# Loading the first matrices in halves, the last expert's tokens in halves, and stages placed anew, in a two-layer attention and expert kernel

## The chip, the cores and the metric

The kernel runs on one core of one Trainium2 chip, in one launch. The metric is the device time of a run in microseconds, lower is better. A core has five instruction queues that run side by side and wait for each other by semaphores: PE (TensorE, matrix products into PSUM), DVE (VectorE), ACT (ScalarE), POOL (GpSimd) and SP (SyncE, here only for issuing transfers). ACT and POOL can issue transfers as well. In the trace, PEld is the loading of PE's weights, which lies beside the products.

## The reference

Eight sequences of 512 tokens with 256 channels (4096 tokens in all) pass through four residual steps, and every step first normalizes its input:

```
x = x + attention0(norm(x), ctx)      # 8 heads of 64, context of 64 tokens with 192 channels, masked
x = x + experts0(norm(x))             # 16 experts of 64, the best 4 of each token, sigmoid weights
x = x + attention1(norm(x), ctx)      # 4 heads of 32, the best 32 keys, FiLM, long convolution, an MLP of 1024, norms
x = x + experts1(norm(x))             # 8 experts of 1024; each takes the 512 tokens that score it highest
```

What the change touches at the start is in attention0: keys are `ctx @ W_k`. The kernel folds queries and keys into one matrix for each sequence and head, `M0 = W_q[head] @ k[head].T`, so that scores are `x @ M0`. What it touches at the end is experts1:

```
vals, idx = top_k(scores.T, 512)          # 512 tokens for each expert
h = gelu(norm(x[idx]) @ fc1 + b1)         # 256 -> 1024
o = (h @ fc2 + b2) * weight               # 1024 -> 256
out = x.at[idx].add(o)                    # added to the tokens' rows
```

## The kernel before

All data is float32. Tokens lie on the 128 partitions; a sequence is 4 tiles of 128 tokens. A program product of float32 shows in the trace as two PE instructions.

**Loads at the start (L341 to L364).** ACT's queue issues `ctxT` (96 partitions, 2 blocks c of 96 channels, 512 columns: 384 KiB), then `wqT` (512 KiB), the mask and `bo`. SP's queue issues `wk` (384 KiB, in `places`), `xT(0)`, `x(0)`, and then weights in the order of need. The trace shows SP and ACT issuing the ninth and later loads only as earlier ones land. DVE forms the sums of `wqT` and scales it (L366 to L369).

**Keys (L371 to L377).** For each block m of 128 of the 512 key rows, `from_context(wk, m)` multiplies the two halves of the context's channels (c = 0 and 1) into one PSUM bank of `ps_m` (two pools of two banks), and ACT (m even) or DVE (m odd) copies it into `kT`. L378 to L385 then form `M0` from `wqT` and `kT` in products of 64 rows.

**The middle (L1310 to L1377).** The four steps of each sequence b are Python generators: `attend0`, `route0`, `experts0`, `attend1`, `convolve`, `dense1`, `settle`, `offer`; `build` prepares the convolution's kernel, mostly on DVE. A list `parts` gives each generator a number of steps and a start and an end in planner's units, and `emit` sorts all steps of all generators by these times. That order is the program's order, from which the framework's scheduler makes each engine's queue; instructions passed to `keep_in_program_order` (called `pin` in the code) keep their order among themselves. `experts0` asks for the routing weights `wB`, spread over the partitions by a transfer, and DVE multiplies them with the products at L803. In `convolve`, DVE's L1059 makes `yv` from the products.

**The last step (L1383 to the end).** A search on DVE and PE finds each expert's tokens. For every expert e, POOL gathers the rows (L1500) and PE transposes them. PE then multiplies with `fc1` in 8 blocks f (`inner`, L1529) and ACT applies GELU from PSUM into `gT` (L1559), at 512 tokens each. For each quarter q of 128 tokens, PE multiplies `gT` with `fc2` (L1562), DVE adds the bias (L1564) and scales (L1565), and POOL adds the rows to `out` by an indirect transfer (L1566). Expert 0 already has its first four blocks in halves of 256 columns, and those are pinned.

Of the kernel before, what the change touches and what calls it, by code (L numbers as in the profile page):

```python
# [21 lines left out]
P = 128  # L22
# [37 lines left out]
def xattn_ffn_two_layers(ctx: ExitStack, tc: tile.TileContext, a: dict, out: bass.AP):  # L60
# [19 lines left out]
    def ps_m(i=None):  # L80
        if i is None:
            turn[0] += 1
            i = turn[0] % 2
        return pm[i].tile([P, 512], F32, name="ps_m")

    def ps_o():
        return po.tile([P, 512], F32, name="ps_o")

    def load(p, name, src, shape, dtype=F32, eng=None):
        t = p.tile(shape, dtype, name=name)  # L90
        (eng or nc.sync).dma_start(t, src)
        return t
# [104 lines left out]
    def mm(ps, pairs):  # L197
        n = len(pairs)
        for i, (lhsT, rhs) in enumerate(pairs):
            nc.tensor.matmul(ps, lhsT, rhs, start=(i == 0), stop=(i == n - 1))  # L200
# [137 lines left out]
    a0t = pool(sl, "a0_t", 2)  # L338
    sv = ExitStack()
    wp = pool(sv, "a0_v")  # L340
    ctxT = load(wp, "ctxT", a["ctxT"].rearrange("(c p) s -> p c s", c=2), [96, 2, B * SC], eng=nc.scalar)  # L341

    wk = places[:96, 12].rearrange("p (c n) -> p c n", c=2)
    nc.sync.dma_start(wk, a["Wk0"].rearrange("(c p) n -> p c n", c=2))
    wqT = places[:, 13].rearrange("p (c n) -> p c n", c=4)
    nc.scalar.dma_start(wqT, a["WqT0"].rearrange("(c p) n -> p c n", p=P))
    load_xT(0)
    load_x(0)
    wv = load(wp, "wv", a["Wv0"].rearrange("(c p) n -> p c n", c=2), [96, 2, 512])
# [21 lines left out]
    def from_context(w, m, i=None):  # L371
        ps = ps_m(i)
        mm(ps, [(w[:, c, m * P : (m + 1) * P], ctxT[:, c, :]) for c in range(2)])
        return ps

    for m in range(4):
        (nc.vector.tensor_copy if m % 2 else nc.scalar.copy)(kT[:, m, :], from_context(wk, m))  # L377
    for hp in range(H0 // 2):  # L378
        for dq in range(2):
            for g in range(2):  # L380
# [412 lines left out]
    def experts0(b):  # L793
        xb = xs[b]
        xT, wBs = routed.pop(b)

        def first(f):
            if f in (2, 4):
                wBs.append(spread(b, len(wBs)))
            wB = wBs[f // 2][:, f % 2]  # L800
            ps = ps_m(1)
            mm(ps, [(keys[:, k, f * P : (f + 1) * P], xT[:, k, :]) for k in range(2)])
            nc.vector.scalar_tensor_tensor(wB, ps, 0.0, wB, ALU.max, ALU.mult)  # L803
            return wB

        for i, acc in enumerate((yield from two_layers(first, vals))):
            pair = xb[:, 2 * i : 2 * i + 2, :]
            nc.vector.tensor_tensor(pair, acc, pair, ALU.add)
            for j in (2 * i, 2 * i + 1):
                n_a1.rows(xb[:, j, :], b * TPB + j)  # L810
        n_a1.close(b)
        nc.sync.dma_start(midr[:, tiles(b), :], xb)
# [413 lines left out]
    def once(action):  # L1226
        action()
        yield
# [92 lines left out]
    for b in range(B):  # L1321
        parts += [
            (attend0(b), 10, b + -0.111, b + 1.0),
            (route[b], 2, b + 1.025, b + 1.04),
            (route[b], 2, b + 1.135, b + 1.601),
            (experts0(b), 17, b + 1.936 + -0.015 * max(b - 5, 0), b + 2.436 + -0.015 * max(b - 5, 0)),
        ]
        if b >= 3:
            parts.append((staged(b), 1, b - 0.9, b - 0.9))
        if b >= 2:  # L1330
            parts.append((staged_T(b), 1, b - 0.6, b - 0.6))
    parts += [(once(convolving), 1, 8.01, 8.01), (once(dense), 1, B + 1.52, B + 1.52)]

    early = (5.5, 7.184, 8.7)
    for b in range(B):
        t = T2 + b
        u = early[b] if b < 3 else t
        v = (8.1, 8.66, 9.952)[b] if b < 3 else t + 1
        n = 0.5 if b < 3 else 1.0
        parts += [  # L1340
            (attends[b], 2, u + -0.02, u + 0.182),
            (attends[b], 8, u + 0.249, u + 0.681),
            (attends[b], 8, u + 0.681, u + 0.938),
            (attends[b], 1, u + 0.933, u + 0.933),
            (attends[b], 1, v - 0.05, v - 0.05),
            (attends[b], 1, v - 0.03, v - 0.03),
            (convs[b], 1, v + 0.035, v + 0.035),
            (convs[b], 4, v + 0.224 * n, v + 0.5 * n),
            (convs[b], 3, v + 0.512 * n, v + 0.605 * n),
            (convs[b], 4, v + 0.597 * n, v + 0.819 * n),  # L1350
        ]
        if b < B - 1:
            parts += [
                (denses[b], 1, t + 2.7, t + 2.7),
                (denses[b], 17, t + 2.718, t + 3.6),
                (settle(b), 5, t + 3.628, t + 3.815),
                (offers[b], 1, t + 4.1 - 0.25 * (b == B - 2), t + 4.1 - 0.25 * (b == B - 2)),
                (offers[b], 1, t + 4.179 - 0.25 * (b == B - 2), t + 4.179 - 0.25 * (b == B - 2)),
            ]
        else:  # L1360


            u = t + 2.46
            parts += [
                (dense1(b, 0), 18, u, u + 0.624),
                (settle(b, 0), 3, u + 0.65, u + 0.65 + 0.05),
                (offer(b, 0), 2, u + 0.72, u + 0.72 + 0.05),
                (dense_last(b, 1), 12, u + 0.61, u + 0.61 + 0.624),
            ]
            for j in js_of(1):  # L1370
                v = u + 0.61 + 0.624 + 0.1 * (j - 2)
                parts += [
                    (settle(b, (j,)), 2, v + 0.01, v + 0.03),
                    (offer(b, (j,)), 2, v + 0.04, v + 0.06),
                ]
    parts.append((once(ending), 1, T2 + B + 1.946, T2 + B + 1.946))
    emit(parts)  # L1377
    s2r.close()

# [130 lines left out]
    for e in range(NE1):  # L1510
        f1, f2 = ns.fcs.pop(e)
        if 0 < e < NE1 - 1:
            lists[e + 1] = listed(e + 1)
        idx, ys = lists.pop(e)

        def affine(dst, src, k):
            nc.scalar.activation(  # L1517
                dst, src, AF.Identity, bias=ns.bet[:, k : k + 1], scale=ns.gam[:, k : k + 1]
            )

        yT = place("yT", e).rearrange("p (k j) d -> p k (j d)", k=2)
        gT = (places[:, 4:8] if e % 2 else places[:, 16:20]).rearrange("p s (f n) -> p (s f) n", n=CAP)
        pss = {}

        def inner(f, cols):
            if f not in pss:
                pss[f] = ps_m()
            for k in range(2):
                ins = nc.tensor.matmul(  # L1529
                    pss[f][:, cols], f1[:, k, f * P : (f + 1) * P], yT[:, k, cols], start=(k == 0), stop=(k == 1)  # L1530
                )
                if cols.stop - cols.start < CAP:
                    pin(ins)

        if e:
            transposed(2, yT, ys, affine)
        else:

            halves = [slice(0, CAP // 2), slice(CAP // 2, CAP)]
            banks = [ps_t(k) for k in range(2)]  # L1540
            for i, cols in enumerate(halves):
                for j in (2 * i, 2 * i + 1):
                    for k, ps in enumerate(banks):
                        y = ys[j][:, k * P : (k + 1) * P]
                        pin(nc.tensor.transpose(ps[:, j * P : (j + 1) * P], y, ident))
                    if j < 2:
                        awake(2)
                for k, ps in enumerate(banks):
                    affine(yT[:, k, cols], ps[:, cols], k)
                for f in range(4):  # L1550
                    inner(f, cols)
            placed(slice(1, NE1))
            lists[1] = listed(1)
        for f in range(NF):
            if f not in pss:
                inner(f, slice(0, CAP))
            ps = pss.pop(f)
            c = e * NF + f
            nc.scalar.activation(gT[:, f, :], ps, AF.Gelu_apprx_tanh, bias=ns.bb1[:, c : c + 1])  # L1559
        for q in range(NQ):  # L1560
            pso = ps_o()
            mm(pso[:, :D], [(gT[:, f, q * P : (q + 1) * P], f2[:, f, :]) for f in range(NF)])  # L1562
            o = wk2.tile([P, D], F32, name="o", bufs=2 * NQ)
            nc.vector.tensor_tensor(o, pso[:, :D], ns.bb2[:, e, :], ALU.add)  # L1564
            nc.vector.tensor_scalar(o, o, ys[q][:, D + e : D + e + 1], None, ALU.mult)  # L1565
            nc.gpsimd.indirect_dma_start(  # L1566
                out=out,
                out_offset=bass.IndirectOffsetOnAxis(ap=idx[:, q : q + 1], axis=0),
                in_=o,
                in_offset=None,  # L1570
                compute_op=ALU.add,
            )
        if e + 2 < NE1:
            ns.fcs[e + 2] = fc_weights(e + 2)
# [124 lines left out]
```

## Time and profile before

| what | us |
|---|---|
| median of 3 runs (lowest, highest) | 1286.02 (1284.69, 1287.09) |
| the profiled execution, its time | 1283.47 |
| its span, first to last instruction | 1281.7 |
| PE busy | 1156.5 (90%) |
| DVE busy | 796.9 (62%) |
| POOL busy | 568.4 (44%) |
| ACT busy | 396.3 (31%) |
| mean granted PE clock | 0.963 |
| wait for the first load at the start | 6.85 |
| last scatter issued at | 1273.85 |

The profile is one execution. Busy shares are means over stages that have different limits, and a busy PE is not a PE at its peak. In a line of the timeline the first number is the start and the second the busy time of the group in it, then engine, line, operation, what it writes and reads, and in brackets the idle time ahead of it and what ended that. In a line of waits stand the total, the number of times and the longest. A line of windows has the busy time and number of instructions of PE, PEld, DVE, ACT and POOL, then the granted PE clock, the share of the DMA engines and GB/s.

### The profile page before, as it was taken

The page shows a single profiled execution, that of the slowest core. Times are in us where ns is not written, and L with a number is a line of the kernel's source. Part 1 is how long each engine was busy: PE and PEld are TensorE (multiplying, and loading weights), DVE is VectorE, ACT ScalarE, POOL GpSimd, SP SyncE. Part 2 cuts the span into 40 slices and gives each one's busy share as a digit, 9 for nine tenths or more (in the row PEclk, how much of TensorE's full clock was granted, in tenths as well). Part 3 has the DMA queues.
Part 4 walks back from the last instruction along what each step waited for, and adds up shares of the span by engine and source line. Part 5 has one row for each costly group of instructions (what it writes and reads, how often), then busy time and mean ns, then how long its engine had stood idle before and what let it go on. Part 6 is the DMA issues. An engine that isn't in the chain of part 4 may idle for free. (4 is left out here: it accounts for less than half of the span.)

```text
span 1281.7 us, 17161 instructions
## 1 busy us (share of the span) xinstructions
PE 1156.5 (90%) x5563; PEld 737.6 (58%) x5563; DVE 796.9 (62%) x3340; ACT 396.3 (31%) x784; POOL 568.4 (44%) x809
## 2 busy tenths in 40 slices
PE   7998989979899989998789999898977799999995
PEld 3555655646566546564445556464655576666663
DVE  4459958847987884698987889795435612211110
ACT  2332222131312330223246355634352022222220
POOL 2333324332342333455596477849763123333331
PEclk9998989989889989999898999999998899999998
DMA  8003314315030223200001101022221024443321
GB/s 256 18 28 84 86 49 115 84 51 132 2 100 11 74 75 84 95 1 17 1 1 50 50 1 35 17 63 72 86 71 34 17 59 115 117 103 100 99 38 17
DMA packets 60783, 80.32 MB, mean 63 GB/s; under 512 B 6035, under 2 KB 45204, under 8 KB 60566
## 3 DMA queue, kind: packets, MB, share of 16 engines
q1 hardware_dynamic: 53142, 69.26, 18.4%
q0 software_dynamic: 6240, 8.79, 4.1%
q10 hardware_dynamic: 1312, 1.18, 0.3%
q8 instruction: 44, 0.72, 0.2%
q14 instruction: 45, 0.37, 0.1%
HBM read 62.04 MB, written 17.17 MB: 62 GB/s over the span
## 5 line engine op out<-in xcount | busy, mean ns | idle before, releaser
L261 PE MATMUL ps_o<-vals,wB 128*128 128x256 f32 x512 | 127.9, 395 | 10.6 <-DVE wB L803 10.6
L200 PE MATMUL ps_m<-xT,keys 128*128 128x512 f32 x256 | 126.2, 620 | 0.0
L261 PEld LDWEIGHTS ps_o<-vals,wB 128*128 128x128 f32 x512 | 98.0, 197 | 38.6 <-DVE wB L803 15.2
L200 PE MATMUL ps_m<-hT,w 128*128 128x512 f32 (+1 forms) x256 | 116.1, 576 | 0.2 <-ACT hT L1084 0.2
L261 PE MATMUL ps_o<-w,gT 128*128 128x256 f32 x480 | 114.4, 380 | 0.1
L1529 PE MATMUL ps_m<-places 128*128 128x512 f32 (+1 forms) x272 | 113.9, 570 | 0.5 <-ACT places L1517 0.5
L200 PE MATMUL ps_o<-places 128*128 128x256 f32 x512 | 114.0, 379 | 0.1
L1566 POOL DMA_INDIRECT out<-o,idx x32 | 51.5, 1610 | 141.0 <-DVE o L1565 73.5
L200 PEld LDWEIGHTS ps_o<-places 128*128 128x128 f32 x512 | 96.6, 190 | 18.4 <-issue 5.7
L261 PEld LDWEIGHTS ps_o<-w,gT 128*128 128x128 f32 x480 | 89.7, 190 | 28.1 <-issue 14.9
L1564 DVE TENSOR_TENSOR o<-ps_o,bb 128x256 f32<-128x256 f32 x32 | 13.6, 425 | 147.1 <-PE ps_o L200 147.1
L972 DVE MATCH_REPLACE8 places<-top,places 128x64 f32<-128x64 f32 x512 | 101.3, 205 | 0.0
L705 POOL TENSOR_TENSOR sc<-sc,mx 128x512 f32<-128x512 f32 x32 | 33.2, 1045 | 119.6 <-DVE mx L704 84.4
L156 DVE BATCH_NORM_STATS2 bnst<-places 128x6 f32<-128x256 f32 x192 | 72.8, 413 | 21.3 <-POOL places L1156 12.8
L1559 ACT ACTIVATE places<-ps_m,bb 128x512 f32<-128x512 f32 x64 | 44.0, 687 | 126.8 <-PE ps_m L1529 126.8
L1529 PEld LDWEIGHTS ps_m<-places 128*128 128x128 f32 x272 | 51.1, 191 | 51.1 <-issue 48.8
L971 DVE MAX8 top<-places 128x8 f32<-128x64 f32 x512 | 79.3, 208 | 0.1
L1042 POOL TENSOR_TENSOR places<-places,t 128x768 f32<-128x768 f32 x32 | 57.5, 1821 | 48.1 <-DVE t L1034 48.0
L200 PEld LDWEIGHTS ps_m<-xT,keys 128*128 128x128 f32 x256 | 49.7, 201 | 43.6 <-issue 40.7
L803 DVE SCALAR_TENSOR_TENSOR wB<-ps_m,wB 128x512 f32<-128x512 f32 x64 | 43.4, 679 | 46.0 <-PE ps_m L200 45.9
L191 PE MATMUL ps_t<-ident,places 128*128 128x128 f32 x256 | 49.4, 288 | 24.8 <-DVE places L722 7.9
L1096 ACT ACTIVATE gT<-ps_m,b 128x512 f32<-128x512 f32 (+1 forms) x64 | 42.1, 657 | 90.4 <-PE ps_m L200 90.1
(369 smaller groups left out, 2238.6 us busy)
## 6 DMA issues: line engine op xcount, KB each, us to landing
wB<-wd SPq DMA_DIRECT2D x64, 256.0 KB, 4.3
places<-in_fc2T SPq DMA_DIRECT2D x8, 1024.0 KB, 5.5
places<-in_fc1T SPq DMA_DIRECT2D x8, 1024.0 KB, 4.9
xT<-in_xT SPq DMA_DIRECT2D x8, 512.0 KB, 3.5
places<-in_x SPq DMA_DIRECT2D x8, 512.0 KB, 3.9
mid_x<-places SPq DMA_DIRECT2D x8, 512.0 KB, 7.2
places<-mid_x SPq DMA_DIRECT2D x8, 512.0 KB, 6.5
tab<-zt SPq DMA_DIRECT2D x7, 528.0 KB, 3.9
```

What stands on the lines that cost most here:

```text
L156: nc.vector.bn_stats(st, src)
L191: nc.tensor.transpose(ps[:, j * P : (j + 1) * P], r[:, k * P : (k + 1) * P], ident)
L200: nc.tensor.matmul(ps, lhsT, rhs, start=(i == 0), stop=(i == n - 1))
L261: nc.tensor.matmul(acc[j // 2][:, (j % 2) * D : (j % 2 + 1) * D], h[:, j * P : (j + 1) * P], rhs[:, f, :], start=(f == 0 and j % 2 == 0), ...
L803: nc.vector.scalar_tensor_tensor(wB, ps, 0.0, wB, ALU.max, ALU.mult)
L971: nc.vector.max(m8, src[:, h, :])
L972: nc.vector.match_replace(wrk[:, h, :], m8, src[:, h, :], -FMAX)
L1042: nc.gpsimd.tensor_tensor(ts[0][:, i], ts[0][:, i], ts[1][:, i], op)
L1096: nc.scalar.activation(g, ps, AF.Gelu, bias=ns.b1[:, f : f + 1])
L1529: ins = nc.tensor.matmul(pss[f][:, cols], f1[:, k, f * P : (f + 1) * P], yT[:, k, cols], start=(k == 0), stop=(k == 1))
L1559: nc.scalar.activation(gT[:, f, :], ps, AF.Gelu_apprx_tanh, bias=ns.bb1[:, c : c + 1])
L1566: nc.gpsimd.indirect_dma_start(out=out, out_offset=bass.IndirectOffsetOnAxis(ap=idx[:, q : q + 1], axis=0), in_=o, in_offset=None, compute ...
```

## The change

Three things are changed. First, `ctxT` and `wk` are each loaded by two transfers, one for each c, the first halves first on ACT's and on SP's queue; `wqT` is split in two, one half on each queue, behind them. The four key banks are opened together, and the products run over all m with c = 0 and then over all m with c = 1, pinned in that order; the copies come after. Second, the last expert (e = 7) makes its first layer on the left 256 tokens for all 8 blocks, then on the right 256 tokens for two blocks, then quarter 0, then the other six right blocks, then quarters 1 to 3, all products pinned; GELU runs on 256 columns there. The other experts keep their form. Third, 14 or so of the planner's numbers are changed.

```diff
-    ctxT = load(wp, "ctxT", a["ctxT"].rearrange("(c p) s -> p c s", c=2), [96, 2, B * SC], eng=nc.scalar)
+    ctxT = wp.tile([96, 2, B * SC], F32, name="ctxT")
     wk = places[:96, 12].rearrange("p (c n) -> p c n", c=2)
-    nc.sync.dma_start(wk, a["Wk0"].rearrange("(c p) n -> p c n", c=2))
     wqT = places[:, 13].rearrange("p (c n) -> p c n", c=4)
-    nc.scalar.dma_start(wqT, a["WqT0"].rearrange("(c p) n -> p c n", p=P))
+    for c in range(2):
+        nc.scalar.dma_start(ctxT[:, c, :], a["ctxT"][96 * c : 96 * c + 96])
+        nc.sync.dma_start(wk[:, c, :], a["Wk0"][96 * c : 96 * c + 96])
+    wqTr = a["WqT0"].rearrange("(c p) n -> p c n", p=P)
+    for c, eng in ((0, nc.scalar), (2, nc.sync)):
+        eng.dma_start(wqT[:, c : c + 2, :], wqTr[:, c : c + 2, :])
...
+    ks = [ps_m(m % 2) for m in range(4)]
+    for c in range(2):
+        for m in range(4):
+            ins = nc.tensor.matmul(
+                ks[m], wk[:, c, m * P : (m + 1) * P], ctxT[:, c, :], start=(c == 0), stop=(c == 1)
+            )
+            tc.keep_in_program_order(ins)
     for m in range(4):
-        (nc.vector.tensor_copy if m % 2 else nc.scalar.copy)(kT[:, m, :], from_context(wk, m))
+        (nc.vector.tensor_copy if m % 2 else nc.scalar.copy)(kT[:, m, :], ks[m])
...
-            (experts0(b), 17, b + 1.936 + -0.015 * max(b - 5, 0), b + 2.436 + -0.015 * max(b - 5, 0)),
+            (experts0(b), 17, b + 1.953 + -0.015 * max(b - 5, 0), b + 2.411 + -0.015 * max(b - 5, 0)),
...
-    early = (5.5, 7.184, 8.7)
+    early = (5.545, 7.184, 8.7)
...
-            (attends[b], 2, u + -0.02, u + 0.182),
+            (attends[b], 2, u + -0.02, u + 0.209),
...
-            (convs[b], 1, v + 0.035, v + 0.035),
-            (convs[b], 4, v + 0.224 * n, v + 0.5 * n),
+            (convs[b], 1, v + 0.086, v + 0.086),
+            (convs[b], 4, v + 0.224 * n, v + 0.474 * n),
...
-            (convs[b], 4, v + 0.597 * n, v + 0.819 * n),
+            (convs[b], 4, v + 0.597 * n, v + 0.839 * n),
...
-                (denses[b], 1, t + 2.7, t + 2.7),
-                (denses[b], 17, t + 2.718, t + 3.6),
+                (denses[b], 1, t + 2.727, t + 2.727),
+                (denses[b], 17, t + 2.718, t + 3.607),
...
-    parts.append((once(ending), 1, T2 + B + 1.946, T2 + B + 1.946))
+    parts.append((once(ending), 1, T2 + B + 1.966, T2 + B + 1.966))
...
-        for f in range(NF):
+        def middle(f, cols):
             if f not in pss:
-                inner(f, slice(0, CAP))
+                inner(f, cols)
+            c = e * NF + f
             ps = pss.pop(f)
-            c = e * NF + f
-            nc.scalar.activation(gT[:, f, :], ps, AF.Gelu_apprx_tanh, bias=ns.bb1[:, c : c + 1])
+            nc.scalar.activation(gT[:, f, cols], ps[:, cols], AF.Gelu_apprx_tanh, bias=ns.bb1[:, c : c + 1])
+
+        whole, left, right = slice(0, CAP), slice(0, CAP // 2), slice(CAP // 2, CAP)
+        if e < NE1 - 1:
+            ahead = [[(f, whole) for f in range(NF)]] + [[]] * (NQ - 1)
+        else:
+            ahead = [[(f, left) for f in range(NF)] + [(f, right) for f in range(2)]]
+            ahead += [[(f, right) for f in range(2, NF)]] + [[]] * (NQ - 2)
         for q in range(NQ):
+            for f, cols in ahead[q]:
+                middle(f, cols)
             pso = ps_o()
-            mm(pso[:, :D], [(gT[:, f, q * P : (q + 1) * P], f2[:, f, :]) for f in range(NF)])
+            for f in range(NF):
+                ins = nc.tensor.matmul(
+                    pso[:, :D], gT[:, f, q * P : (q + 1) * P], f2[:, f, :], start=(f == 0), stop=(f == NF - 1)
+                )
+                if e == NE1 - 1:
+                    pin(ins)
```

Not shown: `early`'s neighbour 9.952 becomes 9.956, and in the last sequence's branch three spans of 0.624 become 0.617.

More of the change, by code (lines that the diff above doesn't have):

```diff
@@ L1337, in xattn_ffn_two_layers @@
         u = early[b] if b < 3 else t
-        v = (8.1, 8.66, 9.952)[b] if b < 3 else t + 1
+        v = (8.1, 8.66, 9.956)[b] if b < 3 else t + 1
         n = 0.5 if b < 3 else 1.0
         parts += [
-            (attends[b], 2, u + -0.02, u + 0.182),
+            (attends[b], 2, u + -0.02, u + 0.209),
             (attends[b], 8, u + 0.249, u + 0.681),
@@ L1364, in xattn_ffn_two_layers @@
             parts += [
-                (dense1(b, 0), 18, u, u + 0.624),
+                (dense1(b, 0), 18, u, u + 0.617),
                 (settle(b, 0), 3, u + 0.65, u + 0.65 + 0.05),
                 (offer(b, 0), 2, u + 0.72, u + 0.72 + 0.05),
-                (dense_last(b, 1), 12, u + 0.61, u + 0.61 + 0.624),
+                (dense_last(b, 1), 12, u + 0.61, u + 0.61 + 0.617),
             ]
             for j in js_of(1):
-                v = u + 0.61 + 0.624 + 0.1 * (j - 2)
+                v = u + 0.61 + 0.617 + 0.1 * (j - 2)
                 parts += [
```

## The prediction

> **What bounds the kernel now.** I read the page first (busy shares and clock), then PE's waits, then the timeline at both ends, where the diff makes its two structural edits.
>
> ```profile
> PE 1156.5 (90%) x5563; PEld 737.6 (58%) x5563; DVE 796.9 (62%) x3340; ACT 396.3 (31%) x784; POOL 568.4 (44%) x809
> ...
> L1566 POOL DMA_INDIRECT out<-o,idx x32 | 51.5, 1610 | 141.0 <-DVE o L1565 73.5
> ```
>
> PE is busy for 90% of the span, so outside its gaps time goes as PE goes: whatever lets PE begin earlier moves all that follows, and whatever delays the last output after PE's last matmul is pure tail. PE's waits name the gaps:
>
> ```profile
> PE ps_o L261 <- DVE wB L803: 10.6, 4, 4.2
> PE ps_m L200 <- DVE yv L1059: 10.4, 6, 4.3
> ...
> PE ps_m L200 <- DMA ctxT<-in_ctxT: 6.8, 1, 6.8
> ```
>
> The last line is the start: nothing runs on PE until the context has landed. The first two are in the stages that the diff places anew. Start of the timeline:
>
> ```profile
> 6.85 9.48 PE L200 MATMUL ps_m<-ctxT,places 96*128 96x512 f32 x16 [6.85 <-DMA ctxT<-in_ctxT]
> ...
> 9.99 1.22 DVE L366 TENSOR_REDUCE sq<-places 128x4 f32<-128x1024 f32 x1 [7.76 <-DMA places<-in_WqT]
> ...
> 15.05 0.65 DVE L377 COPY places<-ps_m 128x512 f32<-128x512 f32 x1
> ...
> 16.26 7.71 PE L200 MATMUL ps_m<-places 64*128 64x512 f32 x32
> ```
>
> The sixteen key instructions (eight products, two instructions each) end at 15.7; their weight loads start 0.86 us apart until 11.28 and 0.43 apart after, so PE runs at half pace for its first 4.4 us. The products of queries and keys follow at 16.26. They need a PSUM bank that DVE's copy of key block 1 sets free at 15.70, and DVE had been busy almost without a break from 9.99, when WqT landed. So the start hangs on two loads: ctxT/Wk for PE, WqT for DVE. What the DMA engines moved meanwhile, by windows of 1 us (last column GB/s):
>
> ```profile
> 2.00:3.00 1.00, 0.00 (x0) 0.00 (x0) 0.23 (x1) 0.00 (x0) 0.83 (x6) 1.00 0.87 139
> 3.00:4.00 1.00, 0.00 (x0) 0.00 (x0) 0.00 (x0) 0.00 (x0) 0.66 (x8) 1.00 0.95 324
> 4.00:5.00 1.00, 0.00 (x0) 0.00 (x0) 0.00 (x0) 0.00 (x0) 0.00 (x0) 1.00 1.07 250
> 5.00:6.00 1.00, 0.00 (x0) 0.00 (x0) 0.00 (x0) 0.00 (x0) 0.00 (x0) 1.00 1.09 229
> 6.00:7.00 1.00, 0.15 (x1) 0.15 (x1) 0.00 (x0) 0.00 (x0) 0.00 (x0) 1.00 1.01 308
> ```
>
> The end of POOL's timeline:
>
> ```profile
> 1244.54 1.55 POOL L1566 DMA_INDIRECT out<-o,idx  x1 [2.98 <-DMA out<-o,idx]
> 1260.22 1.55 POOL L1566 DMA_INDIRECT out<-o,idx  x1 [14.14 <-DVE o L1565]
> 1264.74 1.55 POOL L1566 DMA_INDIRECT out<-o,idx  x1 [2.97 <-DVE o L1565]
> 1269.38 1.55 POOL L1566 DMA_INDIRECT out<-o,idx  x1 [3.10 <-DMA out<-o,idx]
> 1273.85 1.55 POOL L1566 DMA_INDIRECT out<-o,idx  x1 [2.92 <-issue]
> ```
>
> The four scatters of an expert all add into `out`, and each waits for the one before: 4.5 us apart. The last expert's first scatter starts only at 1260.22, since the planner mixed its quarters so that two finish together (DVE L1564 x2 at 1258.83). The rows of the last quarter are ready at 1267.3 (DVE L1565 at 1266.98, 0.35 us), but its scatter starts at 1273.85: 6.5 us of chain alone. After that come 7.85 us (landing, closing), which nothing here touches.
>
> **Part by part.** *Loads in halves.* Two loads of 384 KiB (786 KB) stood first on their queues; the windows sum to 0.75 MB by 5.0 us (34 KB before 2.0), so 786 KB had moved at about 5.2, and they landed at 6.4 and 6.8: some 1.4 us after the bytes. Half of them (393 KB) had moved at 3.7; with the same 1.4 the first halves land at 5.1. PE begins 1.75 us earlier. Bounds: 0, if the halves finish no sooner than the whole, and 3.1 (6.85 less 3.7, no completion time). I take 1.75, since both ends of it are rows. The second halves land at 6.8 as before, and the four products of c = 0 (eight instructions, 3.4 us even at 0.43 each) cover that wait. Each extra load costs its queue 0.4 us of issue (ctxT's row, 0.42), hidden because the engines are busy without a break from 2 us. WqT now shares both queues right behind: 786 + 524 = 1310 KB had moved at 7.1, landing 8.5 instead of 9.95, so DVE's chain begins 1.45 earlier. x(0) and the mask now come after seven or eight loads in flight; the ninth of the trace (the second mask) was issued at 6.43, when the first load had landed, so x(0) may be issued at 5.1 instead of 2.25. Its bytes stand behind xT(0) anyway; it lands near 12.4 as before (SP waited for it then). Key products c by c cost the same sixteen instructions. All four banks are held until c = 1, and the copies come later in the row: block 0 is complete after instruction ten instead of two, near 11.9 by the old spacing, and ACT copied it at 11.64; it is needed only at 14.5, so nothing is lost. Start term: the smaller of 1.75 (PE) and 1.45 (DVE), so **1.45 us**; its bounds are a loss of 0.7 (x(0) later than before by as much as two of its statistics take, 0.35 each, with the copies behind them) and 1.75.
>
> *A rule against the halves.* The Trainium skill (DMA: Bandwidth & Descriptors, Anatomy of one DMA) gives a DMA, there one of the software path, about 2.0 us fixed plus bytes over 436 GB/s: by that estimate a half would land only 0.45 us before a whole, and the sum below would be 1.0 us smaller. The row of 384 KiB shows 6.0 us where that rule gives 2.9, because the loads share the engines, so I keep the bytes. The page TensorE: Matmul & The Clock Gate (The HAM clock gate) says that the window that releases the clock runs freely: if the full pace came at 11.3 whatever PE does before, sixteen instructions from 5.1 would end at 15.1, and the start would give 0.6, not 1.45.
>
> *Last expert in halves.* Its first layer starts at 1238.42. An instruction of 512 columns takes 0.43 us (loads 0.43 apart there); the same line with 256 columns ran for expert 0: sixteen in 3.4 us, 0.2145 each, weight loads of 0.19 beneath. So 32 instructions for the left half, 8 for two right blocks and 16 for quarter 0 take 56 × 0.2145 = 12.0: DVE has it at 1250.4, two operations (0.42 + 0.35) and their starts make 1251.3, and POOL is free (previous scatter 1244.54 + 4.5 = 1249.0). Quarter 1 follows after 24 + 16 instructions: 8.6 later, ready 1259.9; then the chain: scatters at 1259.9, 1264.4 (rows ready 1263.3) and 1268.9 (rows ready 1266.8). Against 1273.85 that is **4.95 us** off the end. GELU on 128x256 has no row: between 0.51 (128x256 affine on ACT, L1517) and 0.69 (128x512, L1559); eight in 6.9 us fit at either. Bounds: if 256 columns cost the 0.234 of expert 0's second half (3.75/16, with a wait in it) quarter 1 comes 1.9 later and 3.0 are left; if no scatter waited, 1273.85 less 1266.8, 7.0. The order is now pinned, so a late GELU of block 7 would hold PE: two right blocks (1.7 us) stand between as cover.
>
> *Stages anew.* The first-layer experts' 17 steps take 0.458 instead of 0.500 units of the planner's time, from 0.017 later; attend1 starts, convolve's first and last steps and dense1 shift by 0.02 to 0.05 (a unit is some 60 us: 16.8 of them reach to the search at 980). Instructions stay the same; only neighbours swap, mostly experts0 against kernel-building steps, whose DVE work stands ahead of the wB products. 8% fewer of those steps inside the window, on gaps of 10.6 us, is **0.9 us**. Bounds: the wB and yv gaps gone, a gain of 21 (10.6 + 10.4); or a new gap like the one at 452.60 to 456.94 (4.3) and its half clock after (the windows 456:468 lose 4.8 of PE's work), a loss of 9.1. I take 0.9, nearest to the rows that the moved steps wait in.
>
> **Sum.** 1.45 + 4.95 + 0.9 = 7.3. The profiled execution took 1283.47 (span 1281.7 + 1.8) and would take 1276.2; it lies 2.6 below the median of the runs, 1286.02, which becomes 1278.7.
>
> **Rivals.** *A, the start is eaten by DVE.* In DVE's queue x(0)'s statistics (12.71, 1.40 us) stand ahead of the key copies. If they stay there, x(0)'s landing at 12.4 and not WqT's sets 16.26; gain 0.3. For: DVE was busy up to the copy. Against: those copies become ready earlier too, and the queue is set anew. Time 1286.0 - 6.15 = 1279.9.
> *B, the end is not freed:* the pinned order makes quarter 0 wait, and quarter 1's rows come no earlier than 1264; the chain of three then ends as before. Time 1286.0 - 2.35 = 1283.7. Against it: expert 0 runs the same halves pinned, at pace.
> *C, the new places close gaps:* half of the 21 us: 1286.0 - 6.4 - 10.5 = 1269.1. Nothing in the page tells which gaps.
> *D, slower:* the experts' steps, set denser, ask for wB before DVE has multiplied it. Priced by the gap at 163.85 to 168.03: 4.2 idle, then 168:172 at clock 0.58, 1.7 of work lost: 5.9 each. One such new gap leaves a gain of 1.4; two, in any of eight batches, give 1286.0 - 7.3 + 11.8 = 1290.5. Against it: the window begins later and the wB copies are issued no later.
>
> **How the numbers follow.** About 0.2% (2.6 us) is what a measurement of this kernel can tell from no change: 1283.4 to 1288.6. Forecast 0.52, A 0.16, B 0.08, C 0.10, D 0.14. Faster: forecast, A, C and a quarter of B, 0.80; same: the rest of B, 0.06; slower: D, 0.14. The range runs from 1271 (near C, whose far half is left out) to 1287 (B and a single gap of D with a weak end); D's two gaps are left out.
>
> **What would show it.** Right: PE's first matmul near 5.1 and the 64-row products near 14.8; L366 near 8.5; the last expert's scatters near 7 us earlier for the first relative to PE's last matmul, and 4.5 us apart from the second on; the last scatter some 2 us behind its rows instead of 6.5. Wrong: first matmul still at 6.8; 512-column pace lost in the halves; or new PE gaps over 2 us between 100 and 950 with clock below 0.7 behind them.

## The result: 3.3 us slower, and the profile after

| | before | after |
|---|---|---|
| median of 20 runs (lowest, highest), us | 1284.48 (1281.44, 1288.31) | 1288.51 (1283.77, 1292.37) |
| ratio to before, 95% interval | | 1.0026 [1.0016, 1.0036] |
| the profiled execution, us | 1283.47 | 1290.54 |
| its span, us | 1281.7 | 1288.8 |
| mean granted PE clock | 0.963 | 0.959 |

The ratio is not the quotient of the medians, which lie 4.0 apart; it makes the change 0.0026 × 1284.48 = 3.3 us slower, where the forecast was 7.3 faster. 1288.51 lies 1.5 above the range's upper end. The two profiled executions differ by 7.1 us, more than the medians: after's lies 2.0 above its median, before's 1.0 below its own. The single traces are therefore read for where time moved, and the ratios for how much. Below, one execution of `e2_end` (4104.97 us) and one of `e7_end_wq_act` (3011.77 us) were slow, for a cause that no run shows; they are counted in the medians of these two kernels and not in the ratios.

On the page of after, PE is busy for 6.7 us longer with 32 instructions more (the halved first layer of the last expert), and its share is still 90%:

```profile
PE 1163.2 (90%) x5595; PEld 747.2 (58%) x5595; DVE 799.1 (62%) x3340; ACT 397.9 (31%) x792; POOL 571.2 (44%) x809
...
L1593 POOL DMA_INDIRECT out<-o,idx x32 | 53.4, 1669 | 138.1 <-DVE o L1592 69.1
```

PE's waits over the whole span of after. The wait for the context is 2.07 shorter than before, and a wait for DVE's L389 (a key copy) is new, of the same size; the wB and yv gaps, which the new places were to relieve, shrank by 2.4 and 0.7:

```profile
PE ps_m L200 <- DVE yv L1071: 9.7, 6, 4.4
PE ps_o L261 <- DVE wB L815: 8.2, 4, 3.2
...
PE ps_m L384 <- DMA ctxT<-in_ctxT: 4.8, 1, 4.8
```

The start of after's timeline. PE begins at 4.78 and DVE's L371 (the sum over WqT) at 7.86. But x(0)'s statistics (L156) begin at 13.34, later than before (12.71), and the key copies (L389) stand behind them. The products of 64 rows begin at 13.71, stop after two instructions, and go on at 16.88, where before they all ran from 16.26:

```profile
4.78 9.00 PE L384 MATMUL ps_m<-ctxT,places 96*128 96x512 f32 x16 [4.78 <-DMA ctxT<-in_ctxT]
...
7.86 1.22 DVE L371 TENSOR_REDUCE sq<-places 128x4 f32<-128x1024 f32 x1 [5.63 <-DMA places<-in_WqT]
...
13.34 1.40 DVE L156 BATCH_NORM_STATS2 bnst<-places 128x6 f32<-128x256 f32 x4 [2.67 <-DMA places<-in_x]
...
13.71 1.12 PE L200 MATMUL ps_m<-places 64*128 64x512 f32 x2
...
16.17 1.25 DVE L389 COPY places<-ps_m 128x512 f32<-128x512 f32 x2
...
16.88 7.70 PE L200 MATMUL ps_m<-places 64*128 64x512 f32 x30 [2.04 <-DVE places L389]
```

The end of POOL's timeline in after. The last expert's four scatters come 8.6, 4.6 and 4.4 us apart, and the last one starts 2.4 after its rows (ready at 1278.64) instead of 6.5:

```profile
1255.99 1.55 POOL L1593 DMA_INDIRECT out<-o,idx  x1 [2.94 <-DMA out<-o,idx]
1263.38 1.55 POOL L1593 DMA_INDIRECT out<-o,idx  x1 [5.84 <-DVE o L1592]
1272.01 1.55 POOL L1593 DMA_INDIRECT out<-o,idx  x1 [7.08 <-DVE o L1592]
1276.64 1.55 POOL L1593 DMA_INDIRECT out<-o,idx  x1 [3.07 <-DMA out<-o,idx]
1281.03 1.55 POOL L1593 DMA_INDIRECT out<-o,idx  x1 [2.84 <-issue]
```

So the end does what it was made for, the start lets PE begin 2.07 earlier and still loses 0.6 at the 64-row products, and the rest of the loss lies between them. PE's first layer of the last expert begins at 1250.00 in after and at 1238.42 before: 11.6 later. From there to the last scatter it is 31.03 instead of 35.43: 4.4 gained. 11.6 - 4.4 = 7.2 is the difference of the spans (7.1). The 11.6 belongs to this pair of traces: in `e2_end` below, with before's order of the queues up to the last expert, that layer begins at 1242.59, 4.2 later than before.

The order of DVE's queue is not the same: in the traces, at 1351 of its 3340 places stands another instruction than before (another line of code, operation or tile). The scheduler makes the queues from simulated times, so there were two candidates for the middle: the moved numbers of the planner, and the earlier start itself, which shifts those simulated times.

### The profile page after: what moved, and what is told of

The parts are those of the page before. It is cut to its first block, busy times and chain, and to the rows that moved or that the text cites. A ratio compares the mean times of both kernels' runs of the same rounds, so it can differ in the third digit from the quotient of the medians.

```text
span 1288.8 us, 17249 instructions
## 1 busy us (share of the span) xinstructions
PE 1163.2 (90%) x5595; PEld 747.2 (58%) x5595; DVE 799.1 (62%) x3340; ACT 397.9 (31%) x792; POOL 571.2 (44%) x809
## 5 line engine op out<-in xcount | busy, mean ns | idle before, releaser
L261 PEld LDWEIGHTS ps_o<-vals,wB 128*128 128x128 f32 x512 | 97.9, 197 | 39.0 <-DVE wB L815 13.4
L1585 PEld LDWEIGHTS ps_o<-places 128*128 128x128 f32 x512 | 96.7, 190 | 16.3 <-issue 3.8
L156 DVE BATCH_NORM_STATS2 bnst<-places 128x6 f32<-128x256 f32 x192 | 73.1, 415 | 25.4 <-POOL places L1168 12.7
L1571 ACT ACTIVATE places<-ps_m,bb 128x512 f32<-128x512 f32 (+1 forms) x72 | 46.1, 640 | 125.8 <-PE ps_m L1541 125.8
L1541 PEld LDWEIGHTS ps_m<-places 128*128 128x128 f32 x304 | 57.2, 191 | 46.8 <-issue 43.0
L1054 POOL TENSOR_TENSOR places<-places,t 128x768 f32<-128x768 f32 x32 | 57.6, 1824 | 51.4 <-DVE t L1046 46.6
L200 PE MATMUL ps_m<-places,eT 128*128 128x256 f32 x256 | 64.1, 396 | 6.7 <-ACT places L661 3.5
```

The costliest lines, as they stand in the source:

```text
L156: nc.vector.bn_stats(st, src)
L261: nc.tensor.matmul(acc[j // 2][:, (j % 2) * D : (j % 2 + 1) * D], h[:, j * P : (j + 1) * P], rhs[:, f, :], start=(f == 0 and j % 2 == 0), ...
L1054: nc.gpsimd.tensor_tensor(ts[0][:, i], ts[0][:, i], ts[1][:, i], op)
L1541: ins = nc.tensor.matmul(pss[f][:, cols], f1[:, k, f * P : (f + 1) * P], yT[:, k, cols], start=(k == 0), stop=(k == 1))
L1571: nc.scalar.activation(gT[:, f, cols], ps[:, cols], AF.Gelu_apprx_tanh, bias=ns.bb1[:, c : c + 1])
L1585: ins = nc.tensor.matmul(pso[:, :D], gT[:, f, q * P : (q + 1) * P], f2[:, f, :], start=(f == 0), stop=(f == NF - 1))
```

## The experiments

**e1_start, e3_places, e4_start_end: the parts of the change.** `e1_start` has only the loads in halves and the key products half by half; `e3_places` only the planner's numbers; `e4_start_end` the start and the last expert's halves with the old numbers. The first lines of the hunk of the start (`e1_start`, `e4_start_end`) and of the numbers (`e3_places`):

```diff
+    for c in range(2):
+        nc.scalar.dma_start(ctxT[:, c, :], a["ctxT"][96 * c : 96 * c + 96])
+        nc.sync.dma_start(wk[:, c, :], a["Wk0"][96 * c : 96 * c + 96])
...
-            (experts0(b), 17, b + 1.936 + -0.015 * max(b - 5, 0), b + 2.436 + -0.015 * max(b - 5, 0)),
+            (experts0(b), 17, b + 1.953 + -0.015 * max(b - 5, 0), b + 2.411 + -0.015 * max(b - 5, 0)),
...
```

> Only the loads in halves and the key products half by half; the old places and the old end. Theory P (the new places cost the middle some 9 to 12 us): the start alone changes little, 0 to +2.5 us, PE's first matmul near 4.8 and the 64-row products held by DVE to about 16.9 as in the changed kernel, and the middle keeps its pace: the first-expert milestones of the second layer stay within 3 us of the kernel before. Theory S (the shifted start makes the scheduler order all queues anew, and that costs the middle): +6 to +12 us, with the loss growing between 250 and 950 us.

> Only the new numbers of the planner; the old start and the old end. Theory P: slower by 8 to 12 us, and the loss grows between 525 and 960 us (convolution, dense layer). Theory S: within 3 us of the kernel before.

> The loads in halves and the last expert in halves, with the old places. Theory P: faster by 2 to 5 us (the end's 4.4 less a start that gains nothing or loses 0.6). Theory S: slower by 3 to 8 us, as the changed kernel.

Medians against 1285.65 of before in the same runs: `e1_start` 1301.82, ratio 1.0127 [1.0101, 1.0153]; `e3_places` 1311.95, 1.0190 [1.0158, 1.0221]; `e4_start_end` 1297.63, 1.0085 [1.0061, 1.0108]. So the start alone costs 16.3 us and the numbers alone 24.4, and together with the end they cost 3.3. Given the new start and the new end, the numbers *gain* 7.6 (1.0085 against 1.0026). The theory that the new places carry the loss (P) falls: they are a repair, for an order that the new start had changed, and by themselves they do harm. Theory S has the sign of the start but not the sizes: it said 6 to 12 for the start alone and at most 3 for the numbers alone. With the start alone, 435 of the 3340 places of DVE's queue hold another instruction, all in the first 57%.

Where `e1_start` loses is a stretch of 160 us, in the lines of windows of before and of `e1_start`. The start's edit lies 490 us ahead of it, and PE is busy for 8.3 us less there, at a lower clock (0.91 for 0.97). PE's stages, about 1 us ahead of before's at 558, are 12 behind at 580 and 16 behind at 640; the traces of `e4_start_end` and `e5_act_copies` have the same two jumps:

```profile
500.00:660.00 160.00, 142.80 (x477) 83.42 (x476) 127.93 (x622) 48.95 (x80) 97.65 (x127) 0.97 0.09 27
```
```profile
500.00:660.00 160.00, 134.46 (x422) 78.41 (x420) 122.62 (x569) 40.15 (x64) 82.97 (x109) 0.91 0.09 26
```

PE's waits in that window, first before's longest one, then those of `e1_start`. Of the two on top, before has none there for `top` and 0.8 for the line of L1054:

```profile
PE ps_m L200 <- DVE yv L1059: 5.7, 2, 4.3
```
```profile
PE ps_m L200 <- DVE top L983: 9.3, 3, 4.9
PE ps_m L200 <- POOL places L1054: 5.3, 2, 2.6
PE ps_m L200 <- DVE yv L1071: 4.9, 2, 4.5
```

The longest of them in `e1_start`'s timelines of PE, DVE and POOL. PE stops from 581.33 to 586.21. The bank that it waits for is released by DVE's L1071 (`yv`, 585.34 to 586.07; the trace names the top-k instruction that follows it). DVE got there late: three weightings of `attend1` (L964) took 5.09 us ahead of it, while POOL added in SBUF for `convolve`:

```profile
586.21 2.04 PE L200 MATMUL ps_m<-F1Fout,amT 128*128 128x512 f32 x2 [4.88 <-DVE top L983]
```
```profile
575.51 5.09 DVE L964 SCALAR_TENSOR_TENSOR places<-places 128x256 f32<-128x256 f32 x3
...
585.34 0.73 DVE L1071 TENSOR_TENSOR yv<-even,ps_m 128x256 f32<-128x256 f32 x2
```
```profile
575.17 3.74 POOL L1054 TENSOR_TENSOR places<-places,t 128x768 f32<-128x768 f32 x2 [2.65 <-DVE t L1046]
578.99 1.33 POOL L1055 TENSOR_TENSOR places<-places 128x512 f32<-128x512 f32 x1
```

All 32 of these weightings, in the groups of before, `e1_start`, `e3_places` and after (busy time, mean ns of one):

```profile
L952 DVE SCALAR_TENSOR_TENSOR places<-places 128x256 f32<-128x256 f32 x32 | 12.6, 424 | 0.0
```
```profile
L964 DVE SCALAR_TENSOR_TENSOR places<-places 128x256 f32<-128x256 f32 x32 | 21.4, 696 | 0.1
```
```profile
L952 DVE SCALAR_TENSOR_TENSOR places<-places 128x256 f32<-128x256 f32 x32 | 20.7, 673 | 0.2
```
```profile
L964 DVE SCALAR_TENSOR_TENSOR places<-places 128x256 f32<-128x256 f32 x32 | 17.3, 555 | 1.0 <-ACT places L990 0.8
```

The same instructions cost DVE 8.8, 8.1 and 4.7 us more in the three slower kernels. In `e1_start` six of them take over 1 us each, three from 575.51 and three from 632.6, at the two jumps of PE's lag. The first three take some 4 us more than they would at 0.42 or less each, while the lag grows by 13: they are a part of that loss, and what the rest is was not separated. Whether POOL's work is why they are slow, `e12_two_inputs` asks below.

**e2_end: the last expert's halves alone.**

```diff
-        for f in range(NF):
+        def middle(f, cols):
...
+            ahead = [[(f, left) for f in range(NF)] + [(f, right) for f in range(2)]]
+            ahead += [[(f, right) for f in range(2, NF)]] + [[]] * (NQ - 2)
```

> Only the last expert in halves; old start, old places. On every engine the order of the queues is that of the kernel before up to the last expert. Theory O (the loss of the changed kernel comes from queues that the scheduler orders anew when the start moves): every stage up to the last expert at its old time within 1 us, and 4.0 to 4.6 us off the end: ratio 0.9965 to 0.997. Theory R (the last expert's pins or halves disturb more than they give): ratio 0.999 or above.

1282.48 against 1286.30: ratio 0.9963 [0.9949, 0.9976], 4.8 us faster. The queues have before's order up to the last expert (DVE's differs at 2 places, POOL's at none), so this is the end's term by itself. The same fact gives a measure for single traces: at equal order, `e2_end`'s profiled execution stands 0.1 us from before's at 120 us and 1 to 4 us from it after 500. Differences of that size between distant stages of two single traces are not read here.

**e5_act_copies, e6_after_act: the four key copies on ACT,** in `e4_start_end` and in after, so that x(0)'s statistics stand ahead of none.

```diff
-        (nc.vector.tensor_copy if m % 2 else nc.scalar.copy)(kT[:, m, :], ks[m])
+        nc.scalar.copy(kT[:, m, :], ks[m])
```

> As the run with the start and the end, but ACT makes all four key copies, so that none of them stands behind x(0)'s statistics on DVE. If DVE's queue is what eats the earlier first matmul: the 64-row products run from about 13.7 us without the 2.0 us gap, and the time is 1.5 to 2.5 us below the run with start and end. If something else holds them (WqT, ACT's table load): the gap stays and the time is equal.

> The changed kernel, with all four key copies on ACT. Its queues keep the changed kernel's order everywhere else. If DVE's queue eats the earlier first product: no gap of 2.0 us at 14.8, and 2 to 4 us faster than the changed kernel, at a ratio of 0.9995 to 1.001 to the kernel before. If not: equal to the changed kernel, 1.0026.

`e5_act_copies` 1293.24, 1.0054 [1.0034, 1.0074] (4.0 less than `e4_start_end`); `e6_after_act` 1285.49, 1.0001 [0.9986, 1.0017] (3.2 less than after). PE's start in `e6_after_act`, where the order of every queue is otherwise after's: the 64-row products run through from 15.43, with no stall:

```profile
4.93 10.57 PE L384 MATMUL ps_m<-ctxT,places 96*128 96x512 f32 x16 [4.93 <-DMA ctxT<-in_ctxT]
15.43 8.00 PE L200 MATMUL ps_m<-places 64*128 64x512 f32 x32
```

They end at 23.43 instead of after's 24.58, 1.15 earlier; the ratios differ by more (0.0025, with intervals of ±0.001 and ±0.0016), so the rest may be scatter. The stall was DVE's queue: rival A of the prediction.

**e7_end_wq_act: another way to the start.** The end in halves, context and keys whole, only WqT in two halves on two queues, copies on ACT.

```diff
-    nc.scalar.dma_start(wqT, a["WqT0"].rearrange("(c p) n -> p c n", p=P))
+    wqTr = a["WqT0"].rearrange("(c p) n -> p c n", p=P)
+    for c, eng in ((0, nc.scalar), (2, nc.sync)):
+        eng.dma_start(wqT[:, c : c + 2, :], wqTr[:, c : c + 2, :])
...
-        (nc.vector.tensor_copy if m % 2 else nc.scalar.copy)(kT[:, m, :], from_context(wk, m))
+        nc.scalar.copy(kT[:, m, :], from_context(wk, m))
```

> The last expert in halves; context and key matrix loaded whole as before, but WqT in two halves on two queues, and all four key copies on ACT; old places. The queues keep the old order beyond the first few instructions. Theory O: the end's 4.4, and 0.5 to 1.0 at the start (64-row products from 15.8 instead of 16.26): ratio 0.9955 to 0.9965, faster than both kernels. Theory R: as for the end alone, 0.999 or above.

1282.70, 0.9962 [0.9947, 0.9977]: what `e2_end` had, and nothing for the start. PE began at 6.88 and its 64-row products at 16.32 (before 16.26), not at the expected 15.8. With whole loads the key products themselves end there, so neither WqT nor the copies bound that version.

**e8_c1_first: the new start in another order.** As `e1_start`, but the products of c = 1 first, which waits for all four halves.

```diff
-    for c in range(2):
+    for c in (1, 0):
...
-                ks[m], wk[:, c, m * P : (m + 1) * P], ctxT[:, c, :], start=(c == 0), stop=(c == 1)
+                ks[m], wk[:, c, m * P : (m + 1) * P], ctxT[:, c, :], start=(c == 1), stop=(c == 0)
```

> The new start with old places and the old end, but the key products begin with c = 1, whose halves land last, so that PE's first product waits for about as long as before. On DVE the order of the queue is the old one up to about 55% of its instructions, and another from there to 95%. Theory O: old times within 2 us up to about 600 us, and a loss or gain of several us that arises only after it. Theory S' (the earlier transfers themselves cost time, whatever the order): the loss of the run with the start alone, +11 us by 560 us, is there again.

1297.90, 1.0085 [1.0071, 1.0099]. PE's first product came at 6.02. DVE's order is before's for the first 55% of the queue, and PE's stages stand 2 to 3 us behind before's up to 629; then the order differs, and they are 16.2 behind at 669 and 14.5 at 970. The halves themselves cost nothing in the middle: the loss stands where the order differs, and here that is another place than in `e1_start`. The weightings cost 12.8 us in this kernel, as before, so this loss is another one; its cause was not followed further.

**e9_one_number, e10_one_number_act, e11_end_one_number: one number.** Of the planner's numbers one was sought that gives DVE's queue before's order with the new start; starting `attend0` 0.009 units earlier does, from 25% of the queue up to the last expert. `e9_one_number` is `e4_start_end` with it, `e10_one_number_act` has the copies on ACT besides. `e11_end_one_number` is the control: the same number with the old start and the new end.

```diff
-            (attend0(b), 10, b + -0.111, b + 1.0),
+            (attend0(b), 10, b + -0.12, b + 1.0),
```

> As the run with start and end, with one number of the planner changed: attend0 starts at b - 0.12 instead of b - 0.111. By that the queues of DVE have the order of the kernel before again from 25% of their instructions on, PE's from 30% on. Theory O (the order alone carries the loss): the loss of 11 us by 565 us is gone, and the time is the end's gain plus a start of 0 to -1: ratio 0.996 to 0.9975 instead of 1.0085. Theory S' (the earlier loads cost time, whatever the order): 1.006 to 1.009.

> The same with all four key copies on ACT. Theory O, with DVE's queue as the start's limit: another 1 to 2 us off, ratio 0.9945 to 0.9965, the fastest of all. Theory S': 1.004 to 1.007.

> Control for the one number: the old start, the last expert in halves, attend0 at b - 0.12. Here the same number gives DVE's queue another order from 55 to 90% of its instructions. Theory O: slower than the run with the end alone (0.9963), by 3 us or more, arising after 600 us. If the number itself is a better place for attend0: as fast as the end alone or faster.

Against 1285.36 of before: `e9_one_number` 1282.69, 0.9974 [0.9959, 0.9988]; `e10_one_number_act` 1279.11 (1275.88 to 1280.43), 0.9941 [0.9921, 0.9961]; `e11_end_one_number` 1293.02, 1.0048 [1.0029, 1.0067]. One number takes `e4_start_end` from 1.0085 to 0.9974, 0.0111 × 1285.5 = 14.3 us, with every load, product and copy as they were. The same number with the old start, where 782 places of DVE's queue hold another instruction than before, costs 10.9 against `e2_end`. So it is no better number in itself: what matters is the order that start and numbers make together. `e10_one_number_act` is faster than both kernels, by 7.6 and by 10.9 us. (The profiled execution of `e9_one_number` took 1287.55, near the highest of its runs, so the trace of the other is read.)

In `e10_one_number_act` PE's work in the stretch that cost `e1_start` 8.3 us is close to before's, its waits there are before's (no `top` among those on top), and the weightings cost what they cost before. The lines of windows, of waits in 500 to 660, and of the groups:

```profile
500.00:660.00 160.00, 141.42 (x463) 81.45 (x462) 125.40 (x619) 48.97 (x80) 94.95 (x126) 0.96 0.09 26
```
```profile
PE ps_m L200 <- DVE yv L1071: 5.7, 2, 4.3
PE ps_m L200 <- ACT qT L926: 2.4, 1, 2.4
```
```profile
L964 DVE SCALAR_TENSOR_TENSOR places<-places 128x256 f32<-128x256 f32 x32 | 12.6, 426 | 0.0
```

Its last scatter starts at 1268.60, 5.25 ahead of before's:

```profile
1268.60 1.55 POOL L1593 DMA_INDIRECT out<-o,idx  x1 [2.97 <-issue]
```

**e12_two_inputs: the disputed cost by itself.** `weigh` is the weighting of 128x256, with both operands in SBUF or with the first in PSUM; `maxima` are MAX8; `sums` are POOL's additions of 128x768 in SBUF, let go by `released`.

```diff
+    weigh(12)
+    maxima(24)
+    weigh(12, ps[:, :D])
+    for part in (lambda: weigh(12), lambda: maxima(40), lambda: weigh(16, ps[:, :D])):
+        released()
+        sums(6)
+        part()
```

> Not the computation of the reference: three forms of DVE instruction of the kernel, first alone, then beside POOL adding 128x768 tiles in SBUF. It asks why DVE's weighting of the 32 best keys (scalar_tensor_tensor of two SBUF operands, 128x256) has a longest record of 2.0 us in the kernels with new starts or new places, and 0.86 in the kernel before. Theory C (what POOL does at that moment slows DVE's instructions with two SBUF operands, so an order that lays them beside POOL's additions costs DVE time): the twelve with two SBUF operands take 0.41 each alone and 1.3 to 2.0 beside POOL; the MAX8 (one SBUF operand, 0.21) and the same instruction with its first operand in PSUM (0.47) keep their time beside POOL. Rival W (those records are long because the instruction waits for its operands, not for POOL's traffic): all three forms take alone and beside POOL the same within 10%. Rival M (POOL slows all of DVE's reads of SBUF): all three forms become slower beside POOL.

The timeline of its one execution, DVE's parts without POOL first, then each beside POOL's additions:

```profile
5.89 4.12 DVE L87 SCALAR_TENSOR_TENSOR ex<-wrk,ex 128x256 f32<-128x256 f32 x12 [5.89 <-DMA wrk<-in_x]
9.91 3.14 DVE L94 MAX8 top<-wrk 128x8 f32<-128x64 f32 x24
12.96 4.05 DVE L87 SCALAR_TENSOR_TENSOR ex<-ps_m,ex 128x256 f32<-128x256 f32 x12
...
18.00 13.74 DVE L87 SCALAR_TENSOR_TENSOR ex<-wrk,ex 128x256 f32<-128x256 f32 x12
18.16 11.61 POOL L98 TENSOR_TENSOR sums<-addend 128x768 f32<-128x768 f32 x6 [17.72 <-DVE addend L102]
...
32.78 5.16 DVE L94 MAX8 top<-wrk 128x8 f32<-128x64 f32 x40
33.01 11.20 POOL L98 TENSOR_TENSOR sums<-addend 128x768 f32<-128x768 f32 x6 [3.24 <-DVE top L94]
...
45.19 5.39 DVE L87 SCALAR_TENSOR_TENSOR ex<-ps_m,ex 128x256 f32<-128x256 f32 x16
```

POOL's six additions end at 29.77, before the twelve weightings beside them do, so 13.74/12 is no price. In narrower windows, one addition with one weighting, then the five weightings that follow POOL's last addition:

```profile
22.09 1.86 POOL L98 TENSOR_TENSOR sums<-addend 128x768 f32<-128x768 f32 x1
22.22 2.02 DVE L87 SCALAR_TENSOR_TENSOR ex<-wrk,ex 128x256 f32<-128x256 f32 x1
```
```profile
29.98 1.75 DVE L87 SCALAR_TENSOR_TENSOR ex<-wrk,ex 128x256 f32<-128x256 f32 x5
```

With two SBUF operands the weightings start 0.34 us apart alone (4.12/12, and 1.75/5 after POOL's end) and take 2.02 us beside POOL: six of them, one for each of POOL's six additions. In `e1_start`, too, three weightings (5.09 us) stand beside three of POOL's additions (3.74 and 1.33). The MAX8 keep 0.13 (3.14/24 and 5.16/40), and the form with an operand in PSUM keeps 0.34 (4.05/12 and 5.39/16). Theory C holds; W and M fall. That is what the Trainium skill says (GPSIMD Engine Reference, Specifications): POOL shares its SBUF interfaces with VectorE and contends with DVE instructions that have two SBUF inputs.

## Why the prediction was wrong, step by step

- **Loads in halves.** PE's first product came at 4.78 (said: 5.1) and L371 at 7.86 (8.5): the bytes of the windows plus 1.4 us of completion were the right estimate. By the rule of the Trainium skill that the prediction weighs (DMA: Bandwidth & Descriptors, Anatomy of one DMA), PE would have begun 0.45 earlier; it was 2.07. The time that the prediction worked out with the page TensorE: Matmul & The Clock Gate (sixteen products ending at 15.1) isn't seen either: they ended at 13.78, and PE's last weight load at half pace came at 8.36, where before it came at 11.28.
- **The start term, 1.45.** It came out as a loss of 0.6 (16.88 against 16.26; in the traces of `e1_start`, `e4_start_end` and `e9_one_number` the products go on still later, at 17.32, 17.96 and 18.56). The failed step is the sentence that x(0) "lands near 12.4 as before": its issue came at 6.01, behind the loads in flight (5.1 was said), and the statistics began at 13.34. The lower bound had this mechanism, x(0) late "with the copies behind them", with a loss of 0.7; rival A had the queue but kept 12.4. With the copies on ACT, the products of 64 rows begin at 15.43, where 14.8 was forecast.
- **Key copies "nothing is lost".** True for PSUM, not for DVE's queue: the key copies of L389 started at 16.17, and all 64-row products but the first two instructions waited for them.
- **The end, 4.95.** Right: 4.4 between the two traces, 4.8 [3.1 to 6.6] in `e2_end`. The scatters' distances (8.63, 4.63, 4.39) were forecast as 8.6, 4.5 and 4.5; quarter 0's scatter came 13.4 after the first layer's start, 12.9 was said, and that 0.5 is the difference. GELU on 128x256 took 0.47, just below its lower bound of 0.51, and hides. Rival B falls.
- **Stages anew, +0.9.** This is the step that failed, and it decides the sign. That "only neighbours swap" was read from the diff of the numbers; 1351 of the 3340 places of DVE's queue hold another instruction. By the ratios the middle lost some 7.5 us: 3.3 in all, with 4.8 gained at the end and 0.6 lost at the start. In this pair of traces it is 11 (11.6, of which 0.6 belongs to the start); in the trace of `e6_after_act`, with after's order, the last expert's first layer begins at 1243.53, 6.5 earlier than in after's, of which 1.15 is its start. The term also had the wrong owner: the new start moves the order as much as the numbers do, and the sum treated the start as a shift that all later work follows unchanged. No term stood for it.
- **Rivals.** D had the right sign and nearly the time (1290.5), but not the mechanism: the wB gaps became smaller, 8.2 for 10.6. The waits that grew belong to `attend1` and `convolve`. In after, DVE spends 4.7 us more on the weightings: three L964 take 4.9 us in all from 623.4 on, beside POOL's L1054 and L1055, and PE's stages, 3.6 us behind before's at 558, are 7.4 behind at 629. How much of the 4.7 reaches PE isn't shown; what adds the other 5 from 629 to 970 in this trace was not separated, nor which of the moved numbers brings it.
- **The range.** Its upper bound for the middle, a loss of 9.1, stood in the working, but the range took in only D with a single gap. With -9.1 for +0.9 the forecast reads 1288.7. That this meets 1288.51 is luck in part, since the same sum counts the start as 1.45 gained.

## What to carry to other kernels

Where a scheduler makes the queues from simulated times, an edit at the start is an edit of the whole order: compare the queues of both programs before a gain is summed up, and when they differ, seek the one number that restores the tuned order instead of judging the edit by its first time. Move planner numbers together with the edit that needs them; numbers tuned for one start cost 11 to 24 us with another. On the engine that feeds PE, keep instructions with two SBUF operands away from POOL's elementwise work, and don't let the copy that PE waits for stand behind one that waits for a later load.

## What the runs showed of the hardware

- DVE's `scalar_tensor_tensor` of two SBUF operands (128x256) runs at 0.34 us a piece alone. Beside POOL's `tensor_tensor` of 128x768 one takes 2.02, and one is done for each of POOL's instructions; single records in the kernels reach 2.0 as well. POOL is slowed only a little by it: 11.61 for six additions, 11.20 beside the other forms.
- Two loads of 384 KiB on two queues let PE begin at 6.85; cut in halves of 192 KiB, the first halves let it begin at 4.78 to 5.18 in the kernels that start with c = 0.
- The middle of the kernel differs by up to 4 us between two executions with the same order of the queues (`e2_end` and before), though the first 120 us agree within 0.1.
